# Two style-modulated convolution stacks and their products on one core: a bank copied by ScalarE, and small matmuls placed between parts of large ones

## The chip, the cores and the metric

The kernel runs on one core of one Trainium2 chip. The metric is the device time of one execution in microseconds. The core has five engines that run side by side, each through its own queue in order: TensorE (PE; its weight loads are listed as PEld), VectorE (DVE), ScalarE (ACT), GpSimd (POOL) and SyncE (SP, which here issues the DMAs). They wait for each other through semaphores. Matmul results land in PSUM, which has eight banks of 128 x 512 fp32; everything else is kept in SBUF.

## The reference

Two layers one after the other, each with a convolution stack ("cond") and a product ("ffn"), added to x of shape (32 samples, 64 channels, 1024 positions):

```python
x = x + L0_ffn(L0_cond(x, cond_512, ...), A, B, Wr)
x = x + L1_ffn(L1_cond(x, cond_512, ...), qweight, scales, zeros, bias)

def cond(x, style, ...):            # four layers: same, upsample, same, downsample
    for i, typ in enumerate(TYPES):
        s = style @ mod_w[i].T + mod_b[i]
        weight = SCALE * w[i] * s[:, None, :, None]              # per sample
        weight = weight * rsqrt(sum(weight ** 2) + EPS)[:, :, None, None]
        x = conv(x, weight, typ) + b[i]        # 3 taps; blurred after "up", before "down"

def L0_ffn(x):                      # x as 2048 tokens of 1024
    scores = x @ Wr.T; top_vals, top_idx = top_k(scores, 16)     # of 64 experts
    G = scatter(softmax(top_vals), top_idx)
    h = einsum('nd,krd->nkr', x, A)                              # rank 16 each
    return 2 * einsum('nkr,kdr->nd', h * G[:, :, None], B)

def L1_ffn(x):                      # W from packed 4-bit numbers
    return x @ (scales * q - zeros) + bias
```

## The kernel before, in words

Samples go in 16 pairs p; a pair is 128 tokens, one token per row (64 channels of each of two samples). Every pair passes, in each of the two layers, through the same stages. The names are those that the profile shows.

| stage | what it does | instructions |
|---|---|---|
| `begin` | loads x of both samples (SP queue), scales it by the style and forms differences (`differences`); composes part of the weights | ACT L566, DVE L567, L568; `composed1`: ACT L477, PE g L482, ACT L491 |
| `conv` (`first`) | the first convolution of one sample | PE c L579 (one bank) and c L585 (two banks), ACT yt L581, DVE L586, memsets L587 and L588, differences DVE L591, POOL L594 |
| `weights` (`composed2`) | the composed weights of the later three convolutions, both samples | PE f L503, ACT copies L515 and L520 (two each), POOL sums L522 and L528 (two each) |
| `later` (`rest`) | the later three convolutions of one sample, by composed weights, into two banks r; their sums give rs; the ends are overwritten (`outer`) | PE r L613 and L621 (bank one), ACT L628 (rt), PE r L631 (bank two), DVE L638, POOL L647, POOL L654 |
| `turn` (`turned`) | turns both rs into tokens and splits them into a high part th (thx) and a low part tl (tlx) | PE t L688, DVE L144 and L661, ACT L662; in layer 0 ACT L666 scales tl and POOL L674 forms td |
| `layer0` | the product with Wr and A in three chunks h, each with limbs thx, tlx (Q) and tdx (D); gates; the gated h go to DRAM | PE h L718, ACT L737 or L739, DVE L740, gates DVE L750 to L762 and ACT L757, POOL L768 |
| `layer0b` | the product with B, in 16 steps of its own, after all pairs of layer 0's first product | PE o L718, ht L812 |
| `layer1` | the product with the unpacked weights in three chunks q, limbs thx and tlx; output rows | POOL L886 (x + bias), PE q L896, DVE L907, L908, L910, POOL L911, SP store L913 |

A first loop runs over k = 0 to 15 (`layer0`), a second over p = 0 to 15 (`layer0b`), a third over the 16 pairs of layer 1. In the first and third loop step k works on three pairs at once: the product of pair k, `later` and `turn` of pair k + 1, `conv` and `weights` of pair k + 2. `layer0` and `layer1` are generators: the loop calls `next(main)` to issue the next part of the product and places the other pair's stages between these calls. Before, the product of a pair stops three times: in layer 1 `later` and `conv` of one sample came together after the first chunk, those of the other sample and `weights` after the second, `turn` after the third. A scheduler then fixes each engine's order, and moves a few matmuls past one another. At k = 2 of the first loop (`ahead`) the small stages come before the product. In the first two steps the weights of layer 0 are split into limbs by DVE L144, ACT L307, POOL L306 and DVE L308 beside the products, and those two pairs use unsplit weights (`WHOLE`).

PSUM: `cps` has three banks for c, r, t and ht; `mps` one bank for g and f; `fps` four banks for products. A stage's matmul waits until the bank it gets has been read by its last reader. In SBUF rs has two buffers, rt one, yt (shared with the scaled sums sc of layer 1) two. The tag `w4` has three buffers, and in layer 1 two of them alternate for the output o; L886 of a pair waits for the store of the pair two before it, and it stands on GpSimd directly behind the last L911 of that pair.

The sum of the second bank before:

```python
done["r0"] = nc.vector.scalar_tensor_tensor(
    r.rearrange("p q i b -> p q (i b)"),
    ps.rearrange("p (q c) -> p q c", q=2),
    a,
    m[:, : 2 * P].unsqueeze(1).to_broadcast([P, 2, 2 * P]),
    ALU.mult, ALU.add,
)
```

Of the kernel before, what the change touches and what calls it, by code (L numbers as in the profile page):

```python
# [15 lines left out]
P = 128  # L16
# [46 lines left out]
def adaln_ffn_kernel(ctx: ExitStack, tc: tile.TileContext, t, out: bass.AP):  # L63
# [535 lines left out]
    def rest(i, n, y, f):  # L599

        a = al3[:, n : n + 1]
        r = wk.tile([P, 2, 2, P], F32, tag="r", name=f"rs{i}_{n}", bufs=2)
        m = wk.tile([P, H], F32, tag="rt", name=f"rt{i}_{n}", bufs=1)

        def w(k):
            return f[:, k * P : (k + 1) * P]

        d = y[:, YD:YO].rearrange("p (a b) -> p a b", a=2)  # L610
        ps = cpst(f"r{i}_{n}_0")
        for j in range(2):
            nc.tensor.matmul(  # L613
                ps[:, : HQ - 1].rearrange("p (i b) -> p i b", i=2),
                w(4 + j),
                y[:, j : j + HQ - 1].rearrange("p (b i) -> p i b", i=2),
                start=(j == 0),
                stop=(j == 1),
            )
        for j in range(2):  # L620
            nc.tensor.matmul(  # L621
                ps[:, (2 + j) * P : (3 + j) * P],
                w(6 + j),
                d[:, j, 1 : HQ - 1 : 2],
                start=True,
                stop=True,
            )
        done["m"] = nc.scalar.activation(m, ps, AF.Identity, bias=csth[:, n : n + 1], scale=a)  # L628
        ps = cpst(f"r{i}_{n}_1")
        for j, k in enumerate((0, 2, 1, 3)):  # L630
            done["r"] = nc.tensor.matmul(  # L631
                ps[:, j * P : (j + 1) * P],
                w(k),
                y[:, YE + j * P : YE + (j + 1) * P],
                start=True,
                stop=True,
            )
        done["r0"] = nc.vector.scalar_tensor_tensor(  # L638
            r.rearrange("p q i b -> p q (i b)"),
            ps.rearrange("p (q c) -> p q c", q=2),  # L640
            a,
            m[:, : 2 * P].unsqueeze(1).to_broadcast([P, 2, 2 * P]),
            ALU.mult,
            ALU.add,
        )
        mid = m[:, 2 * P :].rearrange("p (q b) -> p q b", q=2)
        nc.gpsimd.tensor_tensor(  # L647
            r, r, mid.unsqueeze(2).to_broadcast([P, 2, 2, P]), ALU.add
        )
        return r  # L650
# [77 lines left out]
    def layer0(p, ws):  # L728

        hs = wk.tile([P, AW], F32, tag="w4", name=f"hs{p}", bufs=3)  # L730
        key = f"x0_{p}"
        whole = p in WHOLE

        def joined(col, w, qd):
            dst = hs[:, col : col + w]
            if whole:
                nc.scalar.copy(dst, qd[0])  # L737
                return
            nc.scalar.activation(dst, qd[0], AF.Copy, scale=1.0 + 1.0 / RADIX)  # L739
            nc.vector.scalar_tensor_tensor(dst, qd[1], -1.0 / RADIX, dst, ALU.mult, ALU.add)  # L740

        ga = tiny.tile([P, E], F32, tag="ga", name=f"ga_{p}")

        def gates():
            s0 = hs[:, :E]
            m0 = tiny.tile([P, 8], F32, tag="m0", name=f"m0_{p}")
            m1 = tiny.tile([P, 8], F32, tag="m1", name=f"m1_{p}")
            s1 = tiny.tile([P, E], F32, tag="s1", name=f"s1_{p}")
            s2 = tiny.tile([P, E], F32, tag="s2", name=f"s2_{p}")
            nc.vector.max(m0, s0)  # L750
            nc.vector.match_replace(s1, m0, s0, LOW)
            nc.vector.max(m1, s1)
            nc.vector.match_replace(s2, m1, s1, LOW)
            nm = tiny.tile([P, 1], F32, tag="nm", name=f"nm_{p}")
            nc.vector.tensor_scalar_mul(nm, m0[:, 0:1], -1.0)
            ex = tiny.tile([P, E], F32, tag="ex", name=f"ex_{p}")
            nc.scalar.activation(ex, s0, AF.Exp, bias=nm)  # L757
            su = tiny.tile([P, 1], F32, tag="su", name=f"su_{p}")
            nc.vector.scalar_tensor_tensor(ga, s2, LOW, ex, ALU.is_equal, ALU.mult)
            nc.vector.reduce_sum(su, ga, axis=AX.X)  # L760
            nc.vector.reciprocal(su, su)
            nc.vector.tensor_scalar_mul(ga, ga, su)  # L762

        def gated(c):
            a, b = CHUNKS[c]
            v = hs[:, E + a * R : E + b * R].rearrange("p (e r) -> p e r", r=R)
            g = ga[:, a:b].unsqueeze(2).to_broadcast([P, b - a, R])
            nc.gpsimd.tensor_tensor(v, v, g, ALU.mult)  # L768

        def chunk(c):  # L770
            a, b = CHUNKS[c]
            w = (b - a) * R + (E if c == 0 else 0)
            col = a * R + (E if c > 0 else 0)
            banks = [fpst(f"h{p}_{c}_{j}")[:, :w] for j in range(1 if whole else 2)]
            return banks, slice(col, col + w)

        def done_with(c, ch):
            product(ch, key, ws, at, D)
            joined(ch[1].start, ch[1].stop - ch[1].start, ch[0])

        two = []
        for c in range(2):
            two.append(chunk(c))
            product(two[c], key, ws, at, Q)
        for c in range(2):
            done_with(c, two[c])
            if c == 0:
                gates()
            yield
        ch = chunk(2)  # L790
        product(ch, key, ws, at, Q)
        done_with(2, ch)
        yield
        for c in range(3):
            gated(c)
        nc.sync.dma_start(hgd[p], hs[:, E:])
# [83 lines left out]
    def layer1(p, wq, aux):  # L880


        x1 = wk.tile([P, L], F32, tag="w4", name=f"xb_{p}", bufs=3)
        nc.sync.dma_start(x1, x1d[p].rearrange("p f j -> p (f j)"))
        o = wk.tile([P, L], F32, tag="w4", name=f"o1_{p}", bufs=3)
        nc.gpsimd.tensor_tensor(  # L886
            o.rearrange("p (j f) -> p j f", f=4),
            x1.rearrange("p (f j) -> p j f", f=4),
            aux[:, 2].rearrange("p (j f) -> p j f", f=4),
            ALU.add,  # L890
        )
        for c in range(3):
            ps = fpst(f"q{p}_{c}")[:, :QC]
            for j, half in enumerate(toks[f"x1_{p}"]):
                for k in range(NC):
                    nc.tensor.matmul(  # L896
                        ps,
                        half[:, k],
                        wq[at(k)][:, c * QC : (c + 1) * QC],
                        start=(k == 0 and j == 0),  # L900
                        stop=(k == NC - 1 and j == 1),
                    )
            a = 2 if c == 0 else 0
            cs = slice(c * QC + a - 2, (c + 1) * QC - 2)
            if c == 0:
                nrs = tiny.tile([P, 1], F32, tag="nrs", name=f"nrs{p}")
                nc.vector.tensor_scalar_mul(nrs, ps[:, 0:1], -1.0)  # L907
                nc.vector.scalar_tensor_tensor(o, aux[:, 1], nrs, o, ALU.mult, ALU.add)  # L908
            s = wk.tile([P, QC], F32, tag="yt", name=f"sc{p}_{c}", bufs=2)[:, : QC - a]
            nc.vector.tensor_tensor(s, ps[:, a:], aux[:, 0, cs], ALU.mult)  # L910
            nc.gpsimd.tensor_tensor(o[:, cs], o[:, cs], s, ALU.add)  # L911
            yield
        nc.sync.dma_start(out[p], o)  # L913
# [94 lines left out]
    for k in range(NP):  # L1008
# [16 lines left out]
                split_weights(araw, AW, range(5), wa, "wa")  # L1025
        if k + 3 < NP and not ahead:
            load(k + 3)
        if k + 1 < NP and not ahead:
            later(k + 1, 0)
            if k + 2 < NP:  # L1030
                conv(k + 2, 0)
        next(main)
        if k + 1 < NP and not ahead:
            later(k + 1, 1)
            if k + 2 < NP:
                conv(k + 2, 1)
        if k + 2 < NP and not ahead:
            weights(k + 2)
        if k == NP - 2:
            load_b(range(5), braw)  # L1040
        next(main)
        if k == 1:
            kept = wk.tile([P, AW], F32, tag="w4", name="kept", bufs=3)
            nc.scalar.copy(kept, araw[7])
            split_weights(araw[:7] + [kept], AW, range(5, NC), wa, "wa")
        if last:
            load_b(range(5, NC), braw)
            hg = load_h(0)
            turned_h(0, hg)
        else:  # L1050
            turn(k + 1)
        run(main)
        if not last:
            crossed(f"x0_{k + 1}")
# [50 lines left out]
    for k in range(NP, 2 * NP):  # L1105
# [1 line left out]
        main = layer1(k - NP, *second)  # L1107
        next(main)
        load(k + 3)
        later(k + 1, 0)  # L1110
        conv(k + 2, 0)
        next(main)
        later(k + 1, 1)
        conv(k + 2, 1)
        weights(k + 2)
        next(main)
        turn(k + 1)
        run(main)
        if k == NP:
            run(ends(1, LAST, NP, block(7, [P, 3 * AW], F32, "room3")))  # L1120
# [44 lines left out]
```

## Time and profile before

| | |
|---|---|
| runs | 1011.35, 1014.98, 1018.83 us; median 1014.98 |
| profiled execution | 1015.04 us; span 1013.3 us from first to last instruction |
| TensorE clock granted, mean | 0.976 |
| busy | PE 940.6, PEld 835.0, DVE 644.5, ACT 368.7, POOL 552.6 us |
| HBM | 87 GB/s over the span |
| first loop, steps between the t at 152.3 and the one at 420.4 us | eleven, 268.1 us |
| third loop, steps between the t at 738.8 and the one at 962.6 us | eleven, 223.8 us |

A row of a timeline gives the start from the beginning of the span, the time until the last of the listed instructions ends, the engine, the line, the operation, what is written <- what is read, shapes and count, and in brackets how long the engine stood idle before and what it waited for. Ends of matmuls are modelled, so neighbouring matmuls overlap in it; their start-to-start times are what to add up. fp32 matmuls are recorded as two, those of the split limbs as one.

### The profile page before, as it was taken

What the parts mean: (1) busy time and instruction counts of PE and PEld (TensorE: products, weight loads), DVE (VectorE), ACT (ScalarE), POOL (GpSimd) and SP (SyncE); (2) the same over time, 40 slices, a digit from 0 to 9 for tenths busy, and PEclk for the clock granted to TensorE, in tenths of its full rate; (3) what the DMA queues carried; (4) which work ended last, traced back from release to release, by engine and by line L of the source; (5) the groups of instructions that cost most, each with busy time, mean ns of one, the idle gap of its engine ahead of it and who ended that gap; (6) DMA issues with size and microseconds to landing.
All of it is one profiled execution on the core that took longest, in us unless ns stands there. A gap on an engine that the chain in (4) does not pass through costs nothing.

```text
span 1013.3 us, 14812 instructions
## 1 busy us (share of the span) xinstructions
PE 940.6 (93%) x5302; PEld 835.0 (82%) x5302; DVE 644.5 (64%) x1293; ACT 368.7 (36%) x659; POOL 552.6 (55%) x714
## 2 busy tenths in 40 slices
PE   5689789999999999989999998998899999999997
PEld 4567689999999999984688887877899889988996
DVE  6765665555555555457975444587577887778764
ACT  4253434444444444323331210262333333333330
POOL 3575755555555555545742222246566667667763
PEclk9899989999999999999999999998999999999999
DMA  5802212222222221153243442342122222222111
GB/s 119 244 17 63 62 42 64 63 63 78 68 63 63 63 63 64 63 179 111 98 161 130 148 147 76 128 148 69 63 73 83 72 83 76 78 69 93 54 63 42
DMA packets 39849, 88.87 MB, mean 88 GB/s; under 512 B 12048, under 2 KB 20496, under 8 KB 39776
## 3 DMA queue, kind: packets, MB, share of 16 engines
q1 hardware_dynamic: 37616, 82.48, 24.9%
q0 software_dynamic: 1200, 4.46, 1.4%
q10 hardware_dynamic: 960, 0.99, 0.3%
q8 instruction: 42, 0.69, 0.3%
q14 instruction: 31, 0.25, 0.1%
HBM read 62.74 MB, written 25.17 MB: 87 GB/s over the span
## 4 chain that ended last, share of the span: by engine, by line
PE 68%; DVE 15%; POOL 6%; issue 6%; ACT 3%; DMA 2%; POOLq 0%; DVEq 0%; SPq 0%; ACTq 0%
PE h L718 14%; PE o L718 13%; PE q L896 11%; PE f L503 7%; PE c L585 6%; PE r L613 4%; PE r L631 3%; PE g L482 3%; DVE rs L638 3%; PE t L688 2%; DVE cv L591 2%; PE c L579 2%; PE r L621 2%; DVE cv L567 1%; DVE hs L740 1%
## 5 line engine op out<-in xcount | busy, mean ns | idle before, releaser
L647 POOL TENSOR_TENSOR rs<-rs,rt 128x512 f32<-128x512 f32 x64 | 84.4, 1318 | 85.5 <-DVE rs L638 84.2
L594 POOL TENSOR_TENSOR cv<-cv 128x256 f32<-128x256 f32 x124 | 78.7, 655 | 79.6 <-DVE cv L591 79.6
L628 ACT ACTIVATE rt<-r,csth,al 128x512 f32<-128x512 f32 x64 | 49.7, 777 | 158.8 <-PE r L621 133.4
L740 DVE SCALAR_TENSOR_TENSOR hs<-h,hs 128x368 f32<-128x368 f32 (+1 forms) x42 | 22.3, 531 | 132.7 <-ACT hs L739 74.8
L585 PE MATMUL c<-cv,c 128*128 128x257 f32 (+1 forms) x256 | 83.9, 413 | 23.8 <-DVE rs L638 17.2
L503 PE MATMUL f<-gs,w1b 128*128 128x192 f32 (+1 forms) x576 | 96.8, 315 | 6.3 <-ACT gs L491 6.0
L503 PEld LDWEIGHTS f<-gs,w1b 128*128 128x128 f32 x576 | 92.4, 200 | 10.4 <-ACT gs L491 6.2
L896 PE MATMUL q<-wq,thx 128*128 128x342 f32 x384 | 80.1, 344 | 1.7 <-ACT thx L662 1.7
L585 PEld LDWEIGHTS c<-cv,c 128*128 128x128 f32 x256 | 45.2, 195 | 43.6 <-DVE rs L638 29.6
L567 DVE SCALAR_TENSOR_TENSOR cv<-cv,sty 128x257 f32<-128x257 f32 x64 | 70.9, 1107 | 3.7 <-ACT cv L566 3.4
L515 ACT COPY cv<-f 64x448 f32<-64x448 f32 x64 | 33.8, 528 | 104.3 <-PE f L503 103.3
L613 PE MATMUL r<-cv 128*128 128x256 f32 x248 | 68.1, 395 | 2.6 <-POOL cv L522 2.6
L896 PE MATMUL q<-wq,tlx 128*128 128x342 f32 x384 | 69.2, 323 | 0.0
L718 PE MATMUL h<-wa,thx 128*128 128x352 f32 (+1 forms) x336 | 66.0, 338 | 2.7 <-ACT thx L662 2.7
L718 PE MATMUL h<-wa,tdx 128*128 128x352 f32 (+1 forms) x336 | 68.1, 340 | 0.0
L886 POOL TENSOR_TENSOR o<-xb,aux 128x1024 f32<-128x1024 f32 x16 | 47.1, 2946 | 37.5 <-DMA out_dram<-o 25.6
L896 PEld LDWEIGHTS q<-wq,thx 128*128 128x128 f32 x384 | 62.5, 191 | 6.0 <-ACT thx L662 4.3
L631 PE MATMUL r<-cv 128*128 128x128 f32 x496 | 67.3, 279 | 0.0
L586 DVE SCALAR_TENSOR_TENSOR cv<-c,al,yt 128x257 f32<-128x257 f32 x124 | 58.4, 476 | 9.1 <-ACT yt L581 4.1
L718 PE MATMUL h<-wa,tlx 128*128 128x352 f32 (+1 forms) x336 | 63.9, 332 | 0.0
L896 PEld LDWEIGHTS q<-wq,tlx 128*128 128x128 f32 x384 | 62.9, 192 | 0.0
L631 PEld LDWEIGHTS r<-cv 128*128 128x128 f32 x496 | 62.6, 196 | 0.0
(273 smaller groups left out, 2168.3 us busy)
## 6 DMA issues: line engine op xcount, KB each, us to landing
cv<-in_x_dram SPq DMA_DIRECT2D x64, 256.0 KB, 3.8
hgd<-hs SPq DMA_DIRECT2D x16, 512.0 KB, 2.6
hg<-hgd SPq DMA_DIRECT2D x16, 512.0 KB, 3.5
x1d<-x SPq DMA_DIRECT2D x16, 512.0 KB, 2.9
cv<-x1d SPq DMA_DIRECT2D x128, 64.0 KB, 2.3
xb<-x1d SPq DMA_DIRECT2D x16, 512.0 KB, 3.2
out_dram<-o SPq DMA_DIRECT2D x16, 512.0 KB, 2.6
cv<-in_x_dram SPq DMA_DIRECT2D x13, 512.0 KB, 4.2
```

What stands on the lines that cost most here:

```text
L503: done["f"] = nc.tensor.matmul(ps[:, j * C : (j + rhs.shape[1]) * C].rearrange("p (a b) -> p a b", b=C), w1b[:, NB - 1 - q], rhs, start=(n ...
L567: nc.vector.scalar_tensor_tensor(xe[:, 0], before, s, xe[:, 1], ALU.mult, ALU.subtract)
L585: done["c"] = nc.tensor.matmul(ps, c0[:, q], xe[:, q, :w_], start=True, stop=True)
L586: nc.vector.scalar_tensor_tensor(d, ps, a, yt[:, :w_], ALU.mult, ALU.add)
L594: nc.gpsimd.tensor_tensor(e[:, :, k], d[:, :, 2 * k : 2 * k + HQ - 2 : 2], d[:, :, 1 : HQ - 1 : 2], ALU.subtract)
L613: nc.tensor.matmul(ps[:, : HQ - 1].rearrange("p (i b) -> p i b", i=2), w(4 + j), y[:, j : j + HQ - 1].rearrange("p (b i) -> p i b", i=2), ...
L628: done["m"] = nc.scalar.activation(m, ps, AF.Identity, bias=csth[:, n : n + 1], scale=a)
L631: done["r"] = nc.tensor.matmul(ps[:, j * P : (j + 1) * P], w(k), y[:, YE + j * P : YE + (j + 1) * P], start=True, stop=True,)
L647: nc.gpsimd.tensor_tensor(r, r, mid.unsqueeze(2).to_broadcast([P, 2, 2, P]), ALU.add)
L718: nc.tensor.matmul(banks[l == 2], toks[key][l][:, k], w[:, cols], start=(k == 0 and l != 1), stop=(k == NC - 1 and l in (2, min(n, 2) - 1)),)
L886: nc.gpsimd.tensor_tensor(o.rearrange("p (j f) -> p j f", f=4), x1.rearrange("p (f j) -> p j f", f=4), aux[:, 2].rearrange("p (j f) -> p j ...
L896: nc.tensor.matmul(ps, half[:, k], wq[at(k)][:, c * QC : (c + 1) * QC], start=(k == 0 and j == 0), stop=(k == NC - 1 and j == 1),)
```

## The change

The second bank of a later convolution is copied to SBUF by ScalarE, with its factor, into rs; VectorE then adds m to rs in place. In `layer0` there are three more points to stop at: after the Q limbs of each of the three chunks. In `layer1` there is one more in each chunk, after the high limb. The first loop now puts one small stage at each of five points (later, conv, later, conv, weights), with `turn` ahead of `weights`; before, they came in pairs. The split of the last weights (k = 1) and the first turn of h (last step) move up with `turn`. The third loop does the same with later, conv, later, conv; then `turn`, and after it `weights`. The second loop is not edited.

```diff
--- before.py
+++ after.py
@@ -635,13 +635,10 @@
                 start=True,
                 stop=True,
             )
-        done["r0"] = nc.vector.scalar_tensor_tensor(
-            r.rearrange("p q i b -> p q (i b)"),
-            ps.rearrange("p (q c) -> p q c", q=2),
-            a,
-            m[:, : 2 * P].unsqueeze(1).to_broadcast([P, 2, 2 * P]),
-            ALU.mult,
-            ALU.add,
+        nc.scalar.activation(r.rearrange("p q i b -> p (q i b)"), ps, AF.Copy, scale=a)
+        v = r.rearrange("p q i b -> p q (i b)")
+        done["r0"] = nc.vector.tensor_tensor(
+            v, v, m[:, : 2 * P].unsqueeze(1).to_broadcast([P, 2, 2 * P]), ALU.add
         )
         mid = m[:, 2 * P :].rearrange("p (q b) -> p q b", q=2)
         nc.gpsimd.tensor_tensor(
@@ -782,6 +779,7 @@
         for c in range(2):
             two.append(chunk(c))
             product(two[c], key, ws, at, Q)
+            yield
         for c in range(2):
             done_with(c, two[c])
             if c == 0:
@@ -789,6 +787,7 @@
             yield
         ch = chunk(2)
         product(ch, key, ws, at, Q)
+        yield
         done_with(2, ch)
         yield
         for c in range(3):
@@ -900,6 +899,8 @@
                         start=(k == 0 and j == 0),
                         stop=(k == NC - 1 and j == 1),
                     )
+                if j == 0:
+                    yield
             a = 2 if c == 0 else 0
             cs = slice(c * QC + a - 2, (c + 1) * QC - 2)
             if c == 0:
@@ -1025,30 +1026,30 @@
                 split_weights(araw, AW, range(5), wa, "wa")
         if k + 3 < NP and not ahead:
             load(k + 3)
-        if k + 1 < NP and not ahead:
-            later(k + 1, 0)
-            if k + 2 < NP:
-                conv(k + 2, 0)
-        next(main)
-        if k + 1 < NP and not ahead:
-            later(k + 1, 1)
-            if k + 2 < NP:
-                conv(k + 2, 1)
+        if last:
+            hg = load_h(0)
+        beside = [] if ahead or last else [(later, k + 1, 0), (later, k + 1, 1)]
         if k + 2 < NP and not ahead:
-            weights(k + 2)
+            beside[1:1] = [(conv, k + 2, 0)]
+            beside += [(conv, k + 2, 1), (weights, k + 2)]
+        for n in range(5):
+            for f, *v in beside[n : n + 1]:
+                f(*v)
+            if n < 4:
+                next(main)
+            if n == 3 and k == 1:
+                kept = wk.tile([P, AW], F32, tag="w4", name="kept", bufs=3)
+                nc.scalar.copy(kept, araw[7])
+                split_weights(araw[:7] + [kept], AW, range(5, NC), wa, "wa")
+            if n == 3 and last:
+                turned_h(0, hg)
+            elif n == 3:
+                turn(k + 1)
         if k == NP - 2:
             load_b(range(5), braw)
         next(main)
-        if k == 1:
-            kept = wk.tile([P, AW], F32, tag="w4", name="kept", bufs=3)
-            nc.scalar.copy(kept, araw[7])
-            split_weights(araw[:7] + [kept], AW, range(5, NC), wa, "wa")
         if last:
             load_b(range(5, NC), braw)
-            hg = load_h(0)
-            turned_h(0, hg)
-        else:
-            turn(k + 1)
         run(main)
         if not last:
             crossed(f"x0_{k + 1}")
@@ -1107,14 +1108,17 @@
         main = layer1(k - NP, *second)
         next(main)
         load(k + 3)
-        later(k + 1, 0)
-        conv(k + 2, 0)
-        next(main)
-        later(k + 1, 1)
-        conv(k + 2, 1)
+        for f, *v in (
+            (later, k + 1, 0),
+            (conv, k + 2, 0),
+            (later, k + 1, 1),
+            (conv, k + 2, 1),
+        ):
+            f(*v)
+            next(main)
+        turn(k + 1)
         weights(k + 2)
         next(main)
-        turn(k + 1)
         run(main)
         if k == NP:
             run(ends(1, LAST, NP, block(7, [P, 3 * AW], F32, "room3")))
```

## The prediction

> **What bounds the kernel now.** I read the page first (busy shares, then the chain of waits), then PE's waits, then the timelines of PE, GpSimd and VectorE over one step of each loop that the change touches.
>
> ```profile
> PE 940.6 (93%) x5302; PEld 835.0 (82%) x5302; DVE 644.5 (64%) x1293; ACT 368.7 (36%) x659; POOL 552.6 (55%) x714
> ...
> PE 68%; DVE 15%; POOL 6%; issue 6%; ACT 3%; DMA 2%; POOLq 0%; DVEq 0%; SPq 0%; ACTq 0%
> ```
>
> PE looks full, but a quarter of the chain that ended last lies elsewhere. In PE's waits one line leads:
>
> ```profile
> engine line waited for: us in total, times, longest us
> PE c L585 <- DVE rs L638: 17.2, 25, 2.8
> ```
>
> The third matmul of a convolution waits for the PSUM bank that VectorE's sum L638 still reads. In layer 1 PE shows it once a step:
>
> ```profile
> 854.82 0.49 PE L503 MATMUL f<-gs,w1b 128*128 128x192 f32 x2
> 856.15 0.70 PE L585 MATMUL c<-cv,c 128*128 128x256 f32 x2 [0.84 <-DVE rs L638]
> 856.69 2.35 PE L503 MATMUL f<-gs,w1b 128*128 128x192 f32 x16
> ```
>
> Why L638 is late stands in the GpSimd timeline of a layer-1 step, and in two rows of VectorE's:
>
> ```profile
> 884.04 0.79 POOL L911 TENSOR_TENSOR o<-o,sc 128x342 f32<-128x342 f32 x1
> 887.64 2.87 POOL L886 TENSOR_TENSOR o<-xb,aux 128x1024 f32<-128x1024 f32 x1 [2.81 <-DMA out_dram<-o]
> 891.67 0.92 POOL L911 TENSOR_TENSOR o<-o,sc 128x340 f32<-128x340 f32 x1 [1.16 <-DVE o L908]
> 892.54 1.29 POOL L647 TENSOR_TENSOR rs<-rs,rt 128x512 f32<-128x512 f32 x1
> ...
> 897.97 1.45 POOL L647 TENSOR_TENSOR rs<-rs,rt 128x512 f32<-128x512 f32 x1
> ...
> 901.67 0.73 POOL L522 TENSOR_TENSOR cv<-cv 128x256 f32<-128x256 f32 x1
> ...
> 904.43 0.79 POOL L911 TENSOR_TENSOR o<-o,sc 128x342 f32<-128x342 f32 x1
> ```
>
> ```profile
> 887.79 3.80 DVE L908 SCALAR_TENSOR_TENSOR o<-aux,nrs,o 128x1024 f32<-128x1024 f32 x1
> 891.51 0.74 DVE L638 SCALAR_TENSOR_TENSOR rs<-r,al,rt 128x512 f32<-128x512 f32 x1
> ```
>
> See a ring. GpSimd ends a step's output (884.83), stands 2.81 us until that store has landed (o has two buffers), runs L886; L908, which takes 1.28 us alone, is held to 3.80 by it; then L638, the convolution, the pieces f (L503), their copies and sums (L522), and L911 again. It is 20.4 us long; PE's own work in it is less. From start-to-start times: 48 products at 0.1575 are 7.56; two later convolutions (r) at 2.26 are 4.52, two first ones (c) at 1.31 are 2.62, f 2.52, g 0.98, t 0.87: 19.07. In layer 0 a step lasts 24.39 (the t at 152.3 and 420.4 are eleven steps apart) against 23.32 of work (72 products 11.83, the rest as above): 1.07 of stall.
>
> **The Trainium skill.** "SBUF — State Buffer", Who interferes with whom: a VectorE instruction with two SBUF inputs and a GpSimd one that reads SBUF block each other, one with a single SBUF input doesn't. The trace agrees: L638 (one input in PSUM) takes 731 to 757 ns always, L567 (two in SBUF) 487 to 2198. "VectorE: DVE Perf Modes", the section on the TRN2 errata, prices an fp32 tensor_tensor at (N+151)/0.96 ns; L591 at N=257 takes 420 for 425. "ScalarE: Activation LUTs", What ACT_TABLE_LOAD costs: about 93 ns per pointer operand; L628 with two takes 777. "TensorE: Matmul & The Clock Gate", Part 1: idleness halves PE's clock for some microseconds. Here a 0.84 us wait does nothing, but:
>
> ```profile
> 718.63 0.61 PE L631 MATMUL r<-cv 128*128 128x128 f32 x4
> 721.95 0.84 PE L448 MATMUL ve<-room,cw 128*128 128x48 f32 x6 [2.71 <-DVE room L434]
> 722.62 0.94 PE L631 MATMUL r<-cv 128*128 128x128 f32 x4
> ```
>
> After 2.71 us the same four matmuls take 0.94 for 0.61, and about 1.3 us is lost before the rate returns.
>
> **The change part by part.**
>
> *Bank and sum.* 64 times L638 (0.740) becomes a ScalarE copy, 0.69 (L628 less one pointer, estimate), and a VectorE add in SBUF, 0.69 (the page's price at N=512). ScalarE is a third busy and frees the bank 0.95 us after the matmuls, so PE's 17.2 us of waiting go. The chain to the transposes grows by one instruction of 0.69 and a handover, and the add now fights GpSimd for the port: it can wait out an instruction of up to 2.87 us, or hold one up by about 0.55.
>
> *Layer 0.* Cover between pieces is now h of 1.3 to 2.7 us, and in the changed program t comes before f, with the last h group behind f. I place a step from its first product at 0: second r ends 13.3; copy 14.5 (behind the gates' exponential), add 15.3, L647 16.6, edge copy L654 17.7; t is due at 19.05, so it doesn't wait, and thx and tlx are ready. One new wait: the transposed tokens are split before f's copies, and the scaling of tlx (1.05) stands ahead of them on ScalarE. L144 starts at 19.31, two L144 and two L661 take 2.5, tlx 1.05, four f copies 2.15: 25.0, which is 1.7 in the next step. g shares f's single bank and was due at 1.28: 0.47 late, with about 0.1 for the restart. Step 23.9, gain 0.49; eleven give -5.4. Bounds: 0 to -12 (no wait at g).
>
> *Start-up and end of layer 0.* While weights are split the three helpers are the limit. The 3.55 us that c waits for L628 at 70 shrinks, as its bank copy stands earlier on ScalarE; against that f of tokens 3 now comes after t, and its sums stand behind 12.5 us of weight splitting on GpSimd (114.5 to 127.1). Together -1, bounds -5 to +4. At the end a third of a chunk covers the last turn of x (1.68 of idle at 440.9) and the first of h (1.95 at 456.3, with slow clock after it): -4, bounds -6 to -1. The 16 steps with B in between only see the bank change at their last step: 0, +-2.
>
> *Layer 1.* The order on GpSimd is nearly the old one, but on PE t now comes BEFORE f, so f waits for the second rs. I follow the ring from the end of f at 0, with rows of the trace:
> - two f copies (start 0.28), then four sums at 0.69 and L911: 1.40 + 2.77 + 0.79 = 4.96. L594 is done by then.
> - store 2.80: 7.76. L886 runs to 10.63.
> - L908 is ready at 7.87 (behind the first add and the row sums), 0.11 after L886, as now (0.15): held, ends 11.7.
> - two L586, two memsets, L567: VectorE reaches the two L591 at 13.1; one L911 (0.9) gets between them. Second L591 ends 14.5. PE's second r waits 1.2 for the first L586's bank, inside this time.
> - L568, the second add and two L594 all need the port: 0.36 + 0.55 + 0.45 + 0.45 from 14.4: 16.3.
> - L647 1.27, held back by a VectorE L567 0.25, L911 0.87, L654 0.19: 18.9. t was due at 17.4 even with that wait: 1.5 idle.
> - half of t 0.43 and f 2.52: 21.9.
> The old ring was 20.35 (223.8 us over the eleven steps from 738.8 to 962.6), because f's matmuls and copies lay beside L647 and L594; now they come after. So +1.58 for eleven steps, +17.4. Bounds: 19.07, PE's work (-14.3), and 23.2 with the slow clock each step (+31.7). If L908 got the port first, VectorE's L567 would wait for L886 instead and I get 21.8: hardly different. In the last steps, t ahead of f and of the last products covers 1.9 us of PE's waits at 995 (t for L654 0.5, q for thx 1.4): -2.
>
> Where the stalls go: what is late next is t, for L654 on GpSimd. Waits added: the copy stands ahead of yt (L581) and x's first scaling (L566) on ScalarE, and the first has the second r behind it; both have slack in the placement. DMA queue: loads of x keep their order; only the first turn's load of h goes out earlier.
>
> Sum on the profiled execution (1015.04 us, span 1013.3 plus 1.7 around it): -1 - 5.4 - 4 + 17.4 - 2 = +5.0, **1020 us**. The median of the runs, 1014.98, is the same number, so nothing is shifted.
>
> **Rivals.**
> - *PE-bound in layer 1.* All waits hidden, 19.07 a step: 1015.0 - 1 - 5.4 - 4 - 14.3 - 2 = 988. For: PE's 93%, and the one old step in which L908 came first (at 908, 1.28 us) took 19.6. Against: that step had f before t.
> - *The ring closes at its old length.* The port waits (2.5 us in my sum) fall kinder: 1015 - 12.4 = 1003. For: summed without any wait the ring is 19.4. Against: GpSimd's back-to-back rows above.
> - *Slower: slow clock at t.* If PE's idleness gathers at t and passes some 2 us (0.84 left no slow matmuls, 2.7 did), f runs at half rate inside the ring, +1.3: eleven times 2.88 is 31.7, 1034. It decides from 2 us on; I place 1.5, and 2.8 if L908 goes first.
> - *The change does not spread.* The program order of the changed kernel shows a product group between r and c in both loops, so no.
>
> **How the numbers follow.** Mine 0.42, slow clock 0.20, old length 0.23, PE-bound 0.12, else 0.03. About 1% is what a measurement of this kernel tells from no change: 1005 to 1025. Faster: PE-bound, three quarters of old length, 0.03 of mine: 0.32. Slower: most of slow clock, 0.07 of mine: 0.25. Same: 0.43. My case alone spans 1012 to 1028; the range reaches to 998 and 1036, leaving out PE-bound and the worst of the clock.
>
> **What would show it.** Right: no PE wait on rs at c; in layer 1 a wait of t for GpSimd's L654 of 1 to 2 us and a step near 21.9; in layer 0 a step near 23.9 with a short wait at g for f's copy; L886 still 2.8 us after L911. Wrong: a layer-1 step under 20.4, or t not waiting; then the ring does not pass through t as I say. Matmuls at twice their length after each t: the slow clock.

## The result: 2.7% slower, and where the profile after shows it

The changed kernel takes 1042.9 us, median of four runs (1039.27 to 1043.6), against 1013.48 us for the kernel before, measured beside it: a ratio of 1.0275, 95% interval 1.0226 to 1.0324. The prediction was 1020.0 us with a range up to 1036. The sign of its sum was right and its main mechanism too; four of its terms missed, all in the same direction, by 23 us together.

In the profiled execution (1043.6 us, span 1041.8) PE does the same work as before, but it fills less of the span. Its row on the page:

```profile
PE 942.1 (90%) x5302; PEld 839.4 (81%) x5302; DVE 633.7 (61%) x1293; ACT 409.9 (39%) x723; POOL 578.1 (55%) x714
```

The waits of PE, as total, count and longest: the line that led before, c for VectorE's L638 (17.2 us), is gone. A new one leads.

```profile
PE t L685 <- POOL rs L651: 24.1, 15, 3.6
...
PE r L613 <- POOL cv L522: 15.3, 3, 9.5
...
PE g L482 <- ACT cv L520: 10.8, 23, 0.9
...
PE r L631 <- DVE cv L586: 8.9, 12, 2.4
```

(In the changed kernel the lines have moved. L638 is now ScalarE's copy and L640 VectorE's sum; L644 is the add on GpSimd, L651 the outer copy, L685 the t, L885 x + bias, L909 VectorE's and L912 GpSimd's part of the output.)

To place the 28.5 us, I took for each kind of matmul the lower quartile of its start-to-start times over the compared traces as its work, and counted what is above it as stall. The sums are stalls in us, between marks that are the same point of the program in both. The sums depend somewhat on what is taken as one kind; together they give the difference of the spans. The last column is the best kernel of the experiments.

| part | before | after | difference | predicted | best |
|---|---|---|---|---|---|
| start, to the t of pair 3 | 49.1 | 52.8 | +3.7 | -1 | 47.2 |
| layer 0, eleven steps | 21.1 | 20.3 | -0.8 | -5.4 | 9.7 |
| end of layer 0, to the first o | 5.4 | 0.6 | -4.8 | -4 | 0.6 |
| steps with B | 11.5 | 12.3 | +0.8 | 0 | 12.2 |
| last step with B, entry of layer 1, to the t of pair 2 | 18.3 | 24.8 | +6.5 | 0 | 18.4 |
| layer 1, eleven steps | 24.1 | 42.4 | +18.3 | +17.4 | 9.5 |
| tail | 5.8 | 10.8 | +5.0 | -2 | 2.8 |
| sum | 135.3 | 164.0 | +28.7 | +5.0 | 100.3 |

A layer-1 step lasts 22.08 us, 21.9 were predicted. PE's timeline at its end: t is due at about 894.6 for its second half and gets it 1.53 us of idle later; only then f may run.

```profile
894.04 0.60 PE L685 MATMUL t<-ident,rs 128*128 128x128 f32 x4
896.17 0.66 PE L685 MATMUL t<-ident,rs 128*128 128x128 f32 x4 [1.53 <-POOL rs L651]
896.66 2.68 PE L503 MATMUL f<-gs,w1b 128*128 128x192 f32 x18
```

GpSimd's rows of the same step are the ring: the last output part, the wait for the store, L885, the first L644 (held by the port), and much later the second L644, an output part, and the outer copy that releases t.

```profile
881.20 0.79 POOL L912 TENSOR_TENSOR o<-o,sc 128x342 f32<-128x342 f32 x1
884.81 2.89 POOL L885 TENSOR_TENSOR o<-xb,aux 128x1024 f32<-128x1024 f32 x1 [2.83 <-DMA out_dram<-o]
887.66 2.25 POOL L644 TENSOR_TENSOR rs<-rs,rt 128x512 f32<-128x512 f32 x1
...
893.46 1.28 POOL L644 TENSOR_TENSOR rs<-rs,rt 128x512 f32<-128x512 f32 x1
894.69 1.09 POOL L912 TENSOR_TENSOR o<-o,sc 128x342 f32<-128x342 f32 x1
895.73 0.38 POOL L651 COPY rs<-re 128x2 f32<-128x2 f32 x1
```

Between these two groups stand ScalarE and VectorE. ScalarE first (in brackets: the one buffer of rt makes its L628 wait for the first L644), then two rows of VectorE: L909 held by L885, and the new sum, which takes 1.09 us here.

```profile
889.94 0.78 ACT L628 ACTIVATE rt<-r,csth,al 128x512 f32<-128x512 f32 x1 [3.68 <-POOL rs L644]
890.62 0.68 ACT L638 ACTIVATE rs<-r,al 128x512 f32<-128x512 f32 x1
```

```profile
885.36 3.43 DVE L909 SCALAR_TENSOR_TENSOR o<-aux,nrs,o 128x1024 f32<-128x1024 f32 x1
...
891.93 1.09 DVE L640 TENSOR_TENSOR rs<-rs,rt 128x512 f32<-128x512 f32 x1
```

In layer 0 a step is 24.39 us as before, where 23.9 were predicted. The new wait of g is 0.79 us of idle (0.94 from start to start), not 0.47. VectorE, ScalarE and PE at one step:

```profile
200.32 0.68 DVE L568 SCALAR_TENSOR_TENSOR cv<-cv,sty 128x256 f32<-128x256 f32 x1
200.91 1.27 DVE L144 TENSOR_SCALAR h<-t 128x512 int32<-128x512 int32 x2
```

```profile
203.42 1.06 ACT L663 ACTIVATE tlx<-tlx 128x1024 fp32r<-128x1024 f32 x1 [0.58 <-DVE tlx L658]
204.38 0.51 ACT L515 COPY cv<-f 64x448 f32<-64x448 f32 x1
...
205.99 0.53 ACT L520 COPY cv<-f 64x448 f32<-64x448 f32 x1
```

```profile
206.57 1.24 PE L482 MATMUL g<-r,w2t 128*128 128x192 f32 x6 [0.79 <-ACT cv L520]
```

The t began at 199.62, but L144 only at 200.91, behind L591 and L568 on VectorE. The order on ScalarE (tlx, then f) is as predicted.

### The profile page after: what moved, and what is told of

It is laid out like the page before. It is cut to its first block, busy times and chain, and to the rows that moved or that the text cites. A ratio compares the mean times of both kernels' runs of the same rounds, so it can differ in the third digit from the quotient of the medians.

```text
span 1041.8 us, 14847 instructions
## 1 busy us (share of the span) xinstructions
PE 942.1 (90%) x5302; PEld 839.4 (81%) x5302; DVE 633.7 (61%) x1293; ACT 409.9 (39%) x723; POOL 578.1 (55%) x714
## 3 DMA queue, kind: packets, MB, share of 16 engines
q1 hardware_dynamic: 37616, 82.48, 24.8%
## 5 line engine op out<-in xcount | busy, mean ns | idle before, releaser
L640 DVE TENSOR_TENSOR rs<-rs,rt 128x512 f32<-128x512 f32 x64 | 51.6, 806 | 170.4 <-ACT rs L638 169.4
L644 POOL TENSOR_TENSOR rs<-rs,rt 128x512 f32<-128x512 f32 x64 | 93.0, 1453 | 85.4 <-DVE rs L640 78.1
L594 POOL TENSOR_TENSOR cv<-cv 128x256 f32<-128x256 f32 x124 | 89.6, 742 | 69.5 <-DVE cv L591 61.3
L628 ACT ACTIVATE rt<-r,csth,al 128x512 f32<-128x512 f32 x64 | 49.7, 777 | 127.3 <-PE r L621 65.2
L503 PE MATMUL f<-gs,w1b 128*128 128x192 f32 (+1 forms) x576 | 88.7, 309 | 0.3 <-DVE room L378 0.3
L503 PEld LDWEIGHTS f<-gs,w1b 128*128 128x128 f32 x576 | 85.9, 195 | 0.9 <-DVE room L378 0.5
L591 DVE TENSOR_TENSOR cv<-cv 128x257 f32<-128x257 f32 x124 | 75.8, 652 | 0.3
L895 PE MATMUL q<-wq,tlx 128*128 128x342 f32 x384 | 74.5, 336 | 0.0
L585 PE MATMUL c<-cv,c 128*128 128x257 f32 (+1 forms) x256 | 69.6, 390 | 5.1 <-ACT rs L638 2.2
L586 DVE SCALAR_TENSOR_TENSOR cv<-c,al,yt 128x257 f32<-128x257 f32 x124 | 54.0, 475 | 32.8 <-ACT yt L581 31.5
L522 POOL TENSOR_TENSOR cv<-cv 128x256 f32<-128x256 f32 x62 | 45.1, 727 | 44.8 <-ACT cv L520 44.8
L885 POOL TENSOR_TENSOR o<-xb,aux 128x1024 f32<-128x1024 f32 x16 | 47.0, 2938 | 38.6 <-DMA out_dram<-o 25.5
L659 ACT CAST thx<-h 128x512 fp32r<-128x512 f32 x60 | 36.5, 618 | 78.5 <-DVE h L144 78.5
L715 PE MATMUL o<-wb,thh 128*128 128x512 f32 x224 | 61.6, 405 | 2.3 <-ACT wb L307 1.7
```

Source lines behind the costliest of these rows:

```text
L503: done["f"] = nc.tensor.matmul(ps[:, j * C : (j + rhs.shape[1]) * C].rearrange("p (a b) -> p a b", b=C), w1b[:, NB - 1 - q], rhs, start=(n ...
L585: done["c"] = nc.tensor.matmul(ps, c0[:, q], xe[:, q, :w_], start=True, stop=True)
L586: nc.vector.scalar_tensor_tensor(d, ps, a, yt[:, :w_], ALU.mult, ALU.add)
L591: nc.vector.tensor_tensor(d[:, k], yo[:, k : k + HQ], yb, ALU.subtract)
L594: nc.gpsimd.tensor_tensor(e[:, :, k], d[:, :, 2 * k : 2 * k + HQ - 2 : 2], d[:, :, 1 : HQ - 1 : 2], ALU.subtract)
L640: done["r0"] = nc.vector.tensor_tensor(v, v, m[:, : 2 * P].unsqueeze(1).to_broadcast([P, 2, 2 * P]), ALU.add)
```

## The experiments

Each kernel is compared with the kernel before on the same chip; steps are from the starts of t. The first four ask which part of the change costs.

**1. The bank edit alone** (`bank_only`): the kernel before with (operands written short, here and below)

```diff
-        done["r0"] = nc.vector.scalar_tensor_tensor(r, ps, a, m, ALU.mult, ALU.add)
+        nc.scalar.activation(r, ps, AF.Copy, scale=a)
+        done["r0"] = nc.vector.tensor_tensor(r, r, m, ALU.add)
```

> The kernel before, with the bank copy by ScalarE and the sum from SBUF alone; all small stages stay where they were. Theory A (the bank edit is good by itself, the loss comes from the new places of the stages): PE's 17.2 us of waiting of c for L638 go, a layer-0 step falls from 24.39 to about 23.5 and a layer-1 step from 20.4 to about 19.6; together some 17 us, about 996 us (988 to 1004). Theory B (the added VectorE instruction shares its port with GpSimd, so the sum comes later and costs what the free bank brings): a layer-1 step stays at 20.2 to 21, layer 0 gains at most 5, time 1005 to 1020. Theory C (the bank edit is what made the changed kernel slower): over 1025 us.

Measured: 1000.99 us, ratio 0.9872 (0.9842 to 0.9902). A layer-1 step is 19.62, a layer-0 step 24.00. So the bank edit is a gain where the stages stand in their old places. Its time fits theory A, except that layer 0 gains 0.4 a step, not 0.9.

**2. The new places alone** (`spread_only`): the changed kernel with the old sum L638.

> The changed kernel with the old sum L638 by VectorE from PSUM: only the new places of the stages. If the new places cause the loss (theory A), a layer-1 step stays near 22 us with t waiting for L651, c or r waits for the bank come back, layer 0 is 24.4 to 25, and the time is 1040 to 1055 us. If the port contention of the new VectorE add was in the ring (theory B), the ring loses 0.7 of an instruction and the contention: 21.3 or less a layer-1 step, 1025 to 1035 us. If the bank edit makes the loss (theory C): 1005 to 1020.

Measured: 1014.36 us, ratio 1.0000 (0.9988 to 1.0013). A layer-1 step is 20.79 (0.41 more than before), a layer-0 step 24.01 (0.38 less). None of the three theories fits both runs: the new places alone cost nothing in sum, the bank edit alone gains 12.6 us, and both together lose 29. It is an interaction. GpSimd's order shows where to look for it. In this kernel the outer copy (L654 here) follows the second add (L647 here) directly; in the changed kernel an output part of 1.09 us has come between them (rows above). And t doesn't wait here at all.

```profile
856.12 1.28 POOL L647 TENSOR_TENSOR rs<-rs,rt 128x512 f32<-128x512 f32 x1
857.47 0.28 POOL L654 COPY rs<-re 128x2 f32<-128x2 f32 x1
```

**3. x + bias later** (`xb_late`):

```diff
+        with tc.issue_after(done["outer"].ins):
             nc.gpsimd.tensor_tensor(o, x1, aux[:, 2], ALU.add)      # L885, here L886
```

> The changed kernel with one edge more: GpSimd's x + bias (L886 in this kernel, L885 in the changed one) is issued behind the outer copy L651 of the second sample, which puts it about 8 us later in a step; nothing else is edited. Ring theory (t waits because GpSimd stands 2.8 us for the store of o ahead of L885, L885 holds up VectorE's L909 and GpSimd's L644, and those make L651 late): the wait of t for L651 goes, the 2.8 us on the store too, L909 takes about 1.3 instead of 3.4; a layer-1 step falls from 22.08 to 19.2 to 20.0 us, over eleven steps and the entry and tail 25 to 35 us, time 1008 to 1020. Rival (t comes too early after the second r in PE's order whatever the store does): t still waits over 1 us, a step 21 or more, time 1030 to 1042.

Measured: 1034.16 us, ratio 1.0191 (1.0131 to 1.0251). The wait on the store is gone and t hardly waits (under 0.3 us in each step), as the ring theory says, but the lost time isn't gone: the late L886 now overlaps the differences that VectorE forms in front of L144. GpSimd, then VectorE (the two L591 take 1.47 us in `o_free`):

```profile
891.00 3.05 POOL L886 TENSOR_TENSOR o<-xb,aux 128x1024 f32<-128x1024 f32 x1
```

```profile
890.91 3.42 DVE L591 TENSOR_TENSOR cv<-cv 128x257 f32<-128x257 f32 x2
894.25 1.27 DVE L144 TENSOR_SCALAR h<-t 128x512 int32<-128x512 int32 x2
```

The tokens come late instead (0.71 us of wait at q for thx, then 1.01 at g). The Trainium skill ("SBUF — State Buffer", Who interferes with whom) has a VectorE instruction with two SBUF inputs contend with a GpSimd instruction that reads SBUF, and this pair of rows agrees with it. So the 3 us of L886 have to be placed with VectorE's work in view.

**4. f ahead of t** (`f_first`), in both loops. In the third:

```diff
             f(*v)
+            if (f, v[1]) == (conv, 1):
+                weights(k + 2)
             next(main)
         turn(k + 1)
-        weights(k + 2)
         next(main)
```

> The changed kernel with the weights stage (f) issued ahead of one more part of the product and of turn, in both loops; t follows f and that part. Ring theory: the f copies, sums, output and store of layer 1 start some 4 us earlier against t, so what is left of the ring is about 17.3 us and PE's own work sets the step: 19.1 to 19.8 in layer 1 instead of 22.08. In layer 0 the f copies stand ahead of the scaling of tlx on ScalarE, so the wait of g (0.94 a step) goes: 23.4 to 23.6 instead of 24.38. At the start the sums of f of tokens 3 no longer stand behind the weight splitting on GpSimd: 5 to 9 us. Together 1042.9 - 30 - 10 - 6 = about 997 us (988 to 1008). Rival (the spreading itself, a part of the product between the stages, makes the waits): layer 1 stays at 21.5 or more, time over 1025.

Measured: 995.03 us, ratio 0.9810 (0.9784 to 0.9837). Layer 0 is 23.33 a step, layer 1 19.87. The new places stay, the bank edit stays; only the order of f and t is turned round, and some 48 us go. On ScalarE in layer 0 the copies of f now stand ahead of the scaling of tlx, and g follows the product without a wait (ScalarE, then PE):

```profile
194.48 0.53 ACT L520 COPY cv<-f 64x448 f32<-64x448 f32 x1
...
198.48 1.06 ACT L663 ACTIVATE tlx<-tlx 128x1024 fp32r<-128x1024 f32 x1 [0.57 <-DVE tlx L658]
```

```profile
196.12 1.58 PE L715 MATMUL h<-wa,tdx 128*128 128x368 f32 x8
197.54 1.14 PE L482 MATMUL g<-r,w2t 128*128 128x192 f32 x6
```

The next four take the ring apart.

**5. The outer copy directly behind the add** (`outer_next`):

```diff
+            with tc.issue_after(done["outer"].ins):
                 nc.gpsimd.tensor_tensor(o[:, cs], o[:, cs], s, ALU.add)   # L912
```

> The changed kernel with one order edge on GpSimd: L912 (output, 1.1 us) is issued behind the outer copy L651, so that L651 follows the second L644 directly; in the changed kernel L912 stands between them. If the ring of layer 1 runs through L644, L651, t and f (theory), every full step loses the 1.0 to 1.1 us of that L912: 22.08 falls to about 21.0 and the time from 1042.9 to about 1030 us (1026 to 1034). If t's wait for L651 only fills time in which PE would wait for something else anyway (rival), the step stays above 21.7 and the time above 1038.

Measured: 1027.05 us, ratio 1.0112 (1.0081 to 1.0142). A step is 21.03: 1.05 less, the length of the part that moved. GpSimd and the t of that step:

```profile
889.46 1.27 POOL L644 TENSOR_TENSOR rs<-rs,rt 128x512 f32<-128x512 f32 x1
890.79 0.27 POOL L651 COPY rs<-re 128x2 f32<-128x2 f32 x1
```

```profile
891.12 0.66 PE L685 MATMUL t<-ident,rs 128*128 128x128 f32 x4 [0.45 <-POOL rs L651]
```

So t's wait for L651 is in the ring of the changed kernel. It also splits the interaction: of the 1.29 us a step by which the changed kernel's 22.08 stands above the 20.79 of `spread_only`, 1.05 are the output part that slipped in; only 0.24 are left for all else that the bank edit does there.

**6. A buffer without a pending store** (`o_free`):

```diff
+        if p % 2:
+            o = tokens("td", f"o1_{p}", F32).rearrange("p a b -> p (a b)")
+        else:
             o = wk.tile([P, L], F32, tag="w4", name=f"o1_{p}", bufs=3)
+        with tc.issue_after(done[f"o{p - 2}"].ins):      # last output part of pair p - 2
             nc.gpsimd.tensor_tensor(o, x1, aux[:, 2], ALU.add)
```

> The changed kernel with every second output o in a buffer that layer 1 doesn't use otherwise (that of td), so that x + bias (L889 here, L885 in the changed kernel) finds a buffer whose store ended a step before; it keeps its place in GpSimd's order by an edge to the last output part of the pair two before. Ring theory with the store as a link: the 2.8 us of GpSimd's wait go, L889 runs while VectorE has nothing for its port, L909 takes 1.3 to 2 instead of 3.4 us, and what is left is the chain from the second r to t (copy 0.7, sum 0.7 to 1.1, L644 1.3, output 1.0, L651 0.3 with handovers, against 4.3 us of PE's work): a layer-1 step of 19.5 to 20.2 instead of 22.08, time about 1016 us (1010 to 1022). Rival (the chain from r to t is too long whatever GpSimd did before it, so the store doesn't matter): 21.3 us or more a step, over 1032.

Measured: 1018.08 us, ratio 1.0015 (0.9999 to 1.0032). A step is 20.52, a little above the 19.5 to 20.2 expected. L889 (L885 before) starts with no wait, and L913 (L909 before) takes 2.04 us in place of 3.43. The store is a link of the ring, worth 1.56 us a step; t still waits 0.80.

```profile
864.97 2.92 POOL L889 TENSOR_TENSOR o<-xb,aux 128x1024 f32<-128x1024 f32 x1
```

```profile
868.85 2.04 DVE L913 SCALAR_TENSOR_TENSOR o<-aux,nrs,o 128x1024 f32<-128x1024 f32 x1
```

```profile
877.65 0.66 PE L685 MATMUL t<-ident,rs 128*128 128x128 f32 x4 [0.80 <-POOL rs L651]
```

**7. Both repairs** (`f_first_o_free`): experiments 4 and 6 in one kernel.

> The kernel f_first with the same free buffer for o. If the 0.8 us a step by which its layer-1 step of 19.86 stands above PE's work (19.07) come from L885 behind the store, holding L909 and with it L586 and the second r, they go: 19.1 to 19.3 a step, time 995 - 8 = about 986 us (982 to 990). If they come from the handovers of the chain itself, nothing changes: 19.7 to 19.9, 993 to 997.

Measured: 981.81 us, ratio 0.9667 (0.9635 to 0.9700); the best version, faster than both kernels. A step is 19.01, the 19.07 of PE's own work within the error of that sum. Its PE row on the page, and t, behind a part of the product, with no wait:

```profile
PE 923.1 (94%) x5302; PEld 835.8 (85%) x5302; DVE 603.0 (62%) x1293; ACT 412.0 (42%) x723; POOL 569.9 (58%) x714
```

```profile
833.04 1.50 PE L899 MATMUL q<-wq,thx 128*128 128x342 f32 x8
834.38 1.03 PE L685 MATMUL t<-ident,rs 128*128 128x128 f32 x8
```

**8. Old places in layer 1** (`l0_f_first`): bank edit, first loop of experiment 4, third loop of the kernel before.

> The bank edit; the first loop of f_first (spread, with f ahead of t); the third loop of the kernel before, with its old places. Theory (the places in layer 1 are worth nothing once the bank is free, those of layer 0 are worth 0.67 us a step, 24.0 against 23.33): layer 0 at 23.33, layer 1 at 19.6 as in bank_only, time 1001 - 8 = 992 to 994 us. Rival (spreading layer 1 with f ahead is worth having, by the entry and the last steps): 996 or more.

Measured: 993.82 us, ratio 0.9776 (0.9751 to 0.9801), steps 23.33 and 19.61. The theory is right: with the store in the ring, the old places in layer 1 are as good as the new ones with f ahead.

The last four fill the table and look at the start.

**9. The kernel before with the free buffer only** (`before_o_free`): the edit of experiment 6 and nothing of the change.

> The kernel before with nothing of the change, but with the free buffer for every second o, so that x + bias (L890 here, L886 in the kernel before) doesn't wait for a store. Theory (c waits for L638 because the same ring, with the store in it, makes L638 late): a layer-1 step of 20.35 falls to 19.2 to 19.6, the wait of c falls to under a third, time about 1003 us (999 to 1006). Rival (c waits because L638 stands behind the other VectorE work whatever GpSimd does): a step of 20.1 or more, time over 1009.

Measured: 1004.13 us, ratio 0.9920 (0.9889 to 0.9952). A step falls from 20.38 to 19.28. The same ring bounded the kernel before. The late bank of L638, at which the change aimed, is one link of it in layer 1: experiment 1 takes out the bank and gets 0.76 us a step, this one the store and gets 1.10. The wait of c falls from 17.2 to 9.0 us in all, not to under a third: it goes altogether in the eleven steps of layer 1 (8.5 us before), but the start, layer 0 and the entry of layer 1 keep some 3 us each.

```profile
PE c L585 <- DVE rs L638: 9.0, 15, 3.0
```

**10. Old places in layer 1 with the free buffer** (`l0_f_first_o_free`).

> The kernel l0_f_first (old places in layer 1) with the free buffer for o. Theory (with the ring gone it doesn't matter where the stages of layer 1 stand, PE's work sets the step): 19.0 to 19.2 a step, time 982 to 986 us, like f_first_o_free at 981.8. Rival (the old places need the store's delay less, or the new ones cover something more): 19.4 to 19.6 a step, 988 to 993.

Measured: 987.51 us, ratio 0.9748 (0.9722 to 0.9774), a step of 19.40. The time lies just below the rival's range, the step is the rival's: without the ring the new places are worth 0.39 a step over the old ones, with f ahead.

**11. New places, old sum, free buffer** (`spread_o_free`).

> The new places with the old sum L638 from PSUM and the free buffer for o. In o_free a layer-1 step is still 20.52, with t waiting. Theory (this rest is the longer chain from the second r to t: copy, sum in SBUF, output part between L644 and L651): with the old sum t hardly waits, 19.2 to 19.6 a step, time 994 to 1001 us. Rival (it is t's place ahead of f alone): 20.2 or more, over 1007.

Measured: 998.51 us, ratio 0.9841 (0.9814 to 0.9869), a step of 19.50. What t still waited in experiment 6 was the longer chain behind the second r, the slipped output part included.

Typical (median) layer-1 steps (us) in one table:

| stages, sum | o waits for the store | o in a free buffer |
|---|---|---|
| old places, L638 | 20.38 (before) | 19.28 (9) |
| old places, copy and sum | 19.62 (1) | 19.40 (10) |
| new places, L638 | 20.79 (2) | 19.50 (11) |
| new places, copy and sum | 22.08 (after) | 20.52 (6) |
| new places, copy and sum, f ahead of t | 19.87 (4) | 19.01 (7) |

**12. The split of weights behind the sums of f** (`split_late`): at k = 1 the split of the last weights is issued after the weights stage.

> The changed kernel, with the split of the last weights of layer 0 (k = 1) issued behind the weights stage instead of ahead of it; nothing else. Theory (PE's 9.5 us wait of r for the sums of f of tokens 3, which stand behind the split on GpSimd, is what the start lost): that wait goes to under 3 us, the t at 154.4 us comes at 148 to 151, and the time is 1036 to 1040 us instead of 1042.9. Rival (the three helpers are the limit of the start, whatever their order): the t stays at 153 to 156, the time within 2 us of 1042.9.

Measured: 1042.25 us, ratio 1.0278 (1.0247 to 1.0310). The time is the rival's; the t comes at 152.0, in neither range. The 9.5 us wait of r for L522 is gone, but PE then waits elsewhere, first for the split itself:

```profile
123.03 0.93 PE L715 MATMUL h<-wa,tdx 128*128 128x352 f32 x2 [3.65 <-DVE wah L144]
```

From the t of pair 2 to the t of pair 3 it takes 37.5 us, against 36.5 in the changed kernel. So a long wait isn't a loss of its own length. But the rival's reason, that the helpers are the limit whatever their order, doesn't hold either: with f ahead of t (experiment 4) this stretch takes 30.8 us. Some 2.5 of the difference are f, which lies ahead of the stretch there; about 3 are the order. In the old places, with the same work between the two marks, the bank edit alone (experiment 1) makes it 32.3 for 37.6.

## Why the prediction was wrong, step by step

- **The bound of the kernel before** was read rightly: GpSimd behind the store, L908 held by L886, L638 late, c late. Experiment 9 takes the store out and gets 1.1 us a step.
- **The ring of layer 1** was right: 21.9 predicted, 22.08 measured, +18.3 us for +17.4. It isn't luck: the waits on its way are as predicted too, 2.83 for 2.80 us at L885 and 1.53 for 1.5 at t. One part of its route was not the only one: besides VectorE's chain L908, L586, L591, the trace shows a branch over the single buffer of rt (first L644, second L628, copy, sum). L638's copy ends at 891.30 and the sum starts at 891.93, so the two branches were within 0.6 us of each other.
- **"Eleven steps"** is the first term that failed. The ring was priced for the eleven steps between two marks, the entry was put at nothing and the tail at -2. They were +6.5 and +5.0.

The tail's reason, that t ahead of f and of the last products would cover waits, was wrong in direction. Its first step, from the t at 982.4 to the one at 1004.4, is one more pass of the ring: 22.09 us, where the kernel before takes 19.26 (962.6 to 981.9). In the last one no product is left that doesn't need t, and t waits longest there. The matmuls after it run slowly, 2.45 us for eight that take 1.41:

```profile
1025.62 1.11 PE L685 MATMUL t<-ident,rs 128*128 128x128 f32 x4 [3.62 <-POOL rs L651]
1026.39 2.45 PE L895 MATMUL q<-wq,tlx 128*128 128x342 f32 x8
1028.67 1.41 PE L895 MATMUL q<-wq,thx 128*128 128x342 f32 x8
```

At the entry most of the loss lies in the step from the t at 708.6 to the one at 740.3: 31.7 us, for 26.3 before (712.6 to 738.8). PE's waits in it are 3.6 us, for 2.7 before. But the granted clock is 0.53 from 717 to 731 us, where before it is 0.76 from 721 to 728; as an estimate from these, 6.6 us of clock are missing for 1.7. So the slow clock, which the prediction held as a rival for the ring alone, came at the entry:

```profile
726.67 1.43 PE L460 MATMUL re<-room,cw 128*128 128x16 f32 x6 [2.16 <-DVE room L434]
727.94 1.20 PE L895 MATMUL q<-wq,tlx 128*128 128x342 f32 x3
728.94 2.12 PE L482 MATMUL g<-r,w2t 128*128 128x192 f32 x6
```

The longer waits ahead of this step (t 2.0 us, r 4.8 for the sums of f) are not the loss: the kernel of experiment 7 has them too (1.7 and 4.8) and its entry is as good as before. How much of the slow clock is the change's doing stays open, since the kernel of experiment 9, with the old places, takes 29.3 us for the same step.

- **Layer 0, -5.4**, was -0.8. The wait of g was priced at 0.47 plus 0.1 and measured 0.94, from start to start. The mis-sized term is the start of L144: I put it at t plus 0.26, and it is t plus 1.29, because L591 and L568 stand ahead of it on VectorE. A second slip hid part of it: I had t 4.27 us ahead of the next step's first product, but t, f and eight products alone are 4.70, and the trace has 4.73. So the wait takes nearly all of the 1.07 us that the bank edit and the spreading could give. Experiment 4 puts the copies of f first and gets that, 24.39 to 23.33.
- **The start, -1**, shows as +3.7, but four executions with identical code up to there (the changed kernel and experiments 3, 5, 6) have the t of pair 3 at 154.4, 155.4, 156.6 and 151.7. This scatter of 5 us is there by the t of pair 2, in steps that the change edits as well, so what they lose stays open. From there on the stretch is 36.5 for 37.6, with f moved into it (2.5 us of PE's work) and eight products out of it (1.3), so it gained some 2 us. That is less than it could: the bank edit alone gains 5.3 there, and with f ahead of t about 3 more come back (see experiment 12).
- **The end of layer 0, -4**, was -4.8.
- **The slow clock at t** was rightly not the forecast for the steps of layer 1: after 1.53 us of idle before t, f takes 2.68 us (rows above), the same as in `o_free` after 0.80.

Some sums are slightly off without moving the forecast: PE's work in a layer-0 step adds up to 23.34, not 23.32, and eleven steps at 19.07 would be 14.1 us less, not 14.3.

Of the 23.7 us between the forecast sum and the measured one, entry and tail are 13.5, layer 0 is 4.6, the start 4.7 (open), the ring itself 0.9.

The prediction saw that f now waits behind t and priced it for layer 1. What it didn't see is that this one order is most of the cost of the whole change: the bank edit alone gains, the new places alone are neutral, and with f ahead of t both together gain. The cheapest cure is an order, not a faster instruction.

## What to carry to other kernels

When a ring of waits sets a step, list which instructions are in it before asking what an edit saves: here the order of two stages was worth 2.2 us a step, the wait that led the list before (c for L638) 0.8. Price a ring for every pass round it, entry and tail included, and look in the new instruction order at what slipped between two of its links. And where a wait leads back to a buffer with a pending store, try the buffer first; here it was worth about 9 us in the kernel before and 25 in the changed one.

## What the runs showed of the hardware that I had not expected

- PE ran slowly after two short waits close together, where one longer one did nothing. In `xb_late` the waits are 0.71 us at q and 1.01 us at g, 1.75 us from start to start, the same in each step; in seven of twelve steps the matmuls after the second took up to twice as long, and the step 23.3 instead of 21.7. The granted clock is 0.55 over 898 to 901.5 us, after such a pair, and 1.00 over 876 to 880, after another. In the changed kernel the wait of 1.53 us in each step (with smaller ones at r and g, 0.6 and 0.2) was never followed by it. The Trainium skill ("TensorE: Matmul & The Clock Gate", Part 1) has the clock follow how busy PE has been recently; no run here tests that, or shows what tells the two cases apart. Two steps of one execution:

```profile
876.64 1.24 PE L482 MATMUL g<-r,w2t 128*128 128x192 f32 x6 [1.01 <-ACT cv L520]
...
898.29 2.25 PE L482 MATMUL g<-r,w2t 128*128 128x192 f32 x6 [1.01 <-ACT cv L520]
```

- Even a copy of two columns on GpSimd can last as long as a VectorE instruction beside it: L651 takes 0.19 us alone, and in `o_free` 1.06 beside L913 (869.87 to 870.93, while L913 runs from 868.85 to 870.89), and so in thirteen more steps.
